# Short-lag products of the second image held back for the last attention chunks and the first ffn group (one Trainium2 core)

## The chip, the cores and the metric

The kernel runs on one core of one Trainium2 chip. The metric is the device time of one execution in microseconds, the median of several runs. The engines are named as in the profile: PE (matrix multiply), PEld (its weight loads), DVE (vector), ACT (scalar), POOL (gpsimd) and SP (the queue that issues most DMAs).

## The reference, cut to what matters

Two images of 128 channels and 64 x 64 positions pass a neighbourhood-attention block (layer 0), then a layer 1 on their 4096 tokens. The change lies in layer 1:

```python
t = t + _L1_attn_ref(_ln_t(t))     # softmax(q q^T / sqrt(128), diagonal masked) q
t = t + _L1_ffn_ref(_ln_t(t), ...) # four branches on 1, 1/2, 1/4, 1/8 of the sequence, mixed by weights
def _stu(u, sigma, phi, Mu, Mpp, Mpm):
    return _compute_spectral(u, sigma, phi, Mpp, Mpm) + _compute_ar_u(Mu, u)
def _compute_ar_u(Mu, u):          # the short lags: three shifted products
    out = jnp.zeros(u.shape[:2] + (Mu.shape[-1],), dtype=u.dtype)
    for i in range(Mu.shape[0]):
        ui = jnp.pad(u, ((0, 0), (i, 0), (0, 0)))[:, :sl]
        out = out + jnp.einsum('btd,de->bte', ui, Mu[i])
    return out
```

`_compute_spectral` is a causal convolution of the tokens with 16 filters, followed by a matrix for each filter.

## The kernel before

Layer 0 takes roughly the first 450 us. Then `attention(0)` and `attention(1)` work the two images. An image's 4096 tokens are eight chunks of 512. The pairs (a, c) with c >= a are taken row by row: `weights` makes the scores (line 899) and their exponentials on ACT (906), `turned` transposes them (913, with a DVE copy that also sums rows, 916), and the products go into `own` (927) and `other` (952). When row a is done, DVE adds `own` to `xa` (931) and `fill(chunk, part)` is told. Rows get shorter: the seventh chunk (CHUNKS[6] = 6) is finished inside the last pair (7, 7), the eighth right behind it.

After each of the four steps of a pair `fill()` issues one step of other work: from the queue `urgent` if it has any, else from `steps`. A step that yields True lets the next queue have its turn in the same call. For each finished chunk `urgent` gets `after(b, c, part)`:

1. transpose the chunk's sum (976), divide by the softmax denominator and add to the tokens `tt` (981);
2. layernorm on DVE (174, 175, 164, 182) with a power on POOL (165), giving z; then a bare True;
3. transpose z (193) and copy it to `zc` on ACT (993);
4. and 5. products with the transform `tr` (1012), copied to `ub` (1014, three buffers) and stored to `us` in DRAM (1001);
6. the rest of the transform (1022, 1028, 1030).

After every fourth chunk a half h of the image is complete and `short_lags(b, h)` is due. It has eight steps: for each parity two steps that transpose four token tiles into `xa` (193 on `tt`, ACT copy 1044), then two products of three lags each on `zc` (1053, six matmuls) that DVE adds to `xa` (1060). For the second image the generator of half 0 is kept back (`kept`) until attention has ended. Its steps then alternate with the steps left over, which are the end of the seventh chunk, the eighth chunk and half 1.

`bank()` gives a PSUM tile from a pool of six, used by all of this. Outside blocks of `manual_schedule` a scheduler orders the instructions of each engine by program order and by its own estimate of when they are ready. [...]

The ffn follows, with PE in program order. `inputs(q)` reads `ut` back from `us` (1301), `blocks(q)` reads filter blocks `ct` (1254). `group()` makes 16 products `pc` (1320) that DVE and ACT copy to `y` (1321), and `project` multiplies them with the filter matrices (1332) into `acc`, which ACT copies to `ob` (1339). Two groups are made before the first projection. The PSUM pools of attention are closed before and new ones opened (`ps_c` of six tiles). The filter matrices are made in `filter_matrices` by DVE additions of weights that DMAs bring (1114, 1117, 1119, 1130 to 1135), as steps of the second attention.

`zc` is one tile in the pools of attention and serves both images. `tt[0]`, the first image's tokens, lives in a pool of its own, closed with them.

Of the kernel before, what the change touches and what calls it, by code (L numbers as in the profile page):

```python
# [8 lines left out]
F32 = mybir.dt.float32  # L9
# [5 lines left out]
P = 128  # L15
NB = 2
T = 4096
TH = T // 2
NT = T // P
# [76 lines left out]
def kernel(  # L96
# [20 lines left out]
    dram = ctx.enter_context(tc.tile_pool(name="dram", bufs=1, space=bass.MemoryType.DRAM))  # L117
    first_ = ExitStack()
    fp = first_.enter_context(tc.tile_pool(name="first", bufs=1))
    ap_ = ExitStack()  # L120
    tp0 = ap_.enter_context(tc.tile_pool(name="l1_t0", bufs=1, side="right"))

# [5 lines left out]


    tt, tok, cm = [None, None], [None, None], [None, None]
    tt[0] = tp0.tile([P, NT, P], F32, name="tt0")
    tok[0] = fp.tile([P, NT, P], F32, name="tok0")
    cm[0] = fp.tile([P, T], F32, name="cm0")

# [721 lines left out]
    with ap_:  # L858
# [17 lines left out]

        zc = tp.tile([P, 2, TH + 1], F32, name="zc")
        nc.gpsimd.memset(zc[:, :, 0:1], 0.0)  # L880

        def attention(b, fill):

# [85 lines left out]
        def after(b, c, part):  # L969

            n0 = 4 * c
            ph, f0 = divmod(n0, FB)
            par, h = divmod(ph, 2)
            pt = bank()
            for j in range(4):
                nc.tensor.transpose(pt[:, j * P : (j + 1) * P], xa[b][:, (n0 + j) * P : (n0 + j + 1) * P], ident)
            rden = sp.tile([P, 4], F32, tag="rden", name="rden")
            nc.vector.tensor_reduce(rden, part[:, n0 : n0 + 4, :], AX.X, ALU.add)
            nc.vector.reciprocal(rden, rden)
            for j in range(4):  # L980
                nc.vector.scalar_tensor_tensor(
                    tt[b][:, n0 + j, :], pt[:, j * P : (j + 1) * P], rden[:, j : j + 1], tt[b][:, n0 + j, :],
                    ALU.mult, ALU.add,
                )
            yield
            z = sp.tile([P, 4, P], F32, tag="z4", name="z4")
            layernorm(z, tt[b][:, n0 : n0 + 4, :])
            yield
            yield True
            pt = bank()  # L990
            transposed(pt, z)
            s0 = 1 + h * (TH // 2)
            nc.scalar.copy(
                zc[:, par, s0 : s0 + TH // 2].rearrange("p (c f) -> p f c", f=FB)[:, f0 : f0 + 4, :],
                pt.rearrange("p (f c) -> p f c", f=4),
            )
            yield
            z2 = z.rearrange("p f d -> p (f d)")

            def store(m0, q, src):  # L1000
                nc.sync.dma_start(
                    out=us[m0 // 2 : (m0 + P) // 2, :, 2 * h + q, f0 : f0 + 4, b, par, :].rearrange(
                        "g r f d -> (g r) f d"
                    ),
                    in_=src.rearrange("p (f d) -> p f d", d=P),
                )

            for m0 in (0, P):
                for q in range(2):
                    rows_ = slice(q * SB, (q + 1) * SB)  # L1010
                    pu = bank()
                    nc.tensor.matmul(pu, lhsT=tr[rows_, h, m0 : m0 + P], rhs=z2[rows_], start=True, stop=True)  # L1012
                    ub = sp.tile([P, 512], F32, tag="ub", name="ub", bufs=3)
                    (nc.scalar.copy if q else nc.vector.tensor_copy)(ub, pu)
                    store(m0, q, ub)
                yield

            banks = [bank() for q in range(2)]
            for i in range(2):
                for q in range(2):  # L1020
                    rows_ = slice(q * SB, (q + 1) * SB)
                    nc.tensor.matmul(
                        banks[q][i * 64 : (i + 1) * 64, 0:256], lhsT=tr[rows_, h, 2 * P : NC],
                        rhs=z2[rows_, i * 256 : (i + 1) * 256], start=True, stop=True,
                    )
            ub = sp.tile([P, 512], F32, tag="ub", name="ub", bufs=3)
            for q in range(2):
                (nc.scalar.copy if q else nc.vector.tensor_copy)(ub[:, q * 256 : (q + 1) * 256], banks[q][:, 0:256])
                for i in range(2):
                    nc.sync.dma_start(  # L1030
                        out=us[P:, :, 2 * h + q, f0 + 2 * i : f0 + 2 * i + 2, b, par, :].rearrange("g r f d -> (g r) f d"),
                        in_=ub[i * 64 : (i + 1) * 64, q * 256 : (q + 1) * 256].rearrange("p (f d) -> p f d", d=P),
                    )
            yield

        def short_lags(b, h):


            for par in range(2):
                n0 = (par * 2 + h) * FB  # L1040
                for f0 in range(0, FB, 4):
                    pt = bank()
                    transposed(pt, tt[b][:, n0 + f0 : n0 + f0 + 4, :])
                    nc.scalar.copy(xa[b][:, (n0 + f0) * P : (n0 + f0 + 4) * P], pt)
                    yield
                xv = xa[b][:, n0 * P : (n0 + FB) * P].rearrange("p (f c) -> p f c", f=FB)
                for c0 in range(0, P, 64):
                    py = bank()
                    for lag in range(3):
                        from_par = (par - lag) % 2  # L1050
                        back = (lag - par + from_par) // 2
                        s0 = 1 + (h * P + c0) * FB - back
                        nc.tensor.matmul(  # L1053
                            py, lhsT=mu[:, lag, :], rhs=zc[:, from_par, s0 : s0 + 512], start=(lag == 0), stop=(lag == 2)
                        )
                    pv = py.rearrange("p (c f) -> p f c", f=FB)
                    first = h == 0 and c0 == 0
                    for lo, hi, s in ((0, 32, 0), (32, 64, 1)) if first else ((0, 64, 2 + h),):
                        xs = xv[:, :, c0 + lo : c0 + hi]
                        nc.vector.scalar_tensor_tensor(  # L1060
                            xs, pv[:, :, lo:hi], seg[:, s : s + 1], xs, ALU.mult, ALU.add
                        )
                    yield
# [74 lines left out]
        def filters():  # L1138
# [44 lines left out]
            for slot in range(begin[-1] + SG):  # L1183
# [4 lines left out]
                    keep(*mj)  # L1188
                yield

        def filler(b, steps, kept=None):

            urgent, done = [], []

            def fill(c=None, part=None):
                if c is not None:
                    done.append(c)
                    urgent.append(after(b, c, part))
                    if len(done) % 4 == 0:
                        held = kept if kept is not None and len(done) == 4 else urgent  # L1200
                        held.append(short_lags(b, len(done) // 4 - 1))
                    return

                for queue in (urgent, steps):
                    while queue:
                        got = next(queue[0], False)
                        if got is None:
                            return
                        if got:
                            break  # L1210
                        queue.pop(0)

            return fill, urgent

# [23 lines left out]
        l1 = ctx.enter_context(tc.tile_pool(name="l1", bufs=1))  # L1238
        mpl = l1.tile([P, KF, P], F32, name="mpl")
        mmi = l1.tile([P, KF, P], F32, name="mmi")  # L1240
        inv = l1.tile([P, 3, CB], F32, name="inv")
        ctp = ctx.enter_context(tc.tile_pool(name="blocks", bufs=5))

# [17 lines left out]
                first_blocks.append(blocks(q))  # L1261
                yield

        steps = [*left, filter_matrices(mpl, mmi), load_blocks()]

        kept = []
        fill, left = filler(1, steps, kept)
# [1 line left out]
        for gen in steps:  # L1269
            for _ in gen:  # L1270
                pass
        kept = kept.pop()
        for gen in left:
            for _ in gen:
                next(kept, None)
        for _ in kept:
            pass

# [7 lines left out]
    outf = out.rearrange("b c h w -> b c (h w)")  # L1288
    with ExitStack() as cv:
        cp = cv.enter_context(tc.tile_pool(name="conv", bufs=5))  # L1290
        obp = cv.enter_context(tc.tile_pool(name="ob", bufs=1))
        ps_c = cv.enter_context(tc.tile_pool(name="ps_c", bufs=6, space=PSUM))
        ps_p = cv.enter_context(tc.tile_pool(name="ps_p", bufs=2, space=PSUM))

        ob = obp.tile([P, 2, NB, FB, 2 * BC, 2], F32, name="ob")
        ob_last = obp.tile([P, 2, NB, FB, BINS - 2 * BC, 2], F32, name="ob_last")

        def inputs(q):

# [4 lines left out]
            )  # L1304
            return ut

        def group():


            y = cp.tile([P, 8, KF, 2, 32], F32, tag="y", name="y", bufs=2)  # L1310
            for q in range(GB // 2):
                ct, ut = ahead.pop(0)
                for par in range(2):

                    cv_ = ct[:, :, 0 : 288 + par * 32].rearrange("p o (l c) -> p o l c", l=2)[:, :, :, 0 : FB * KF]
                    for b in range(NB):
# [44 lines left out]
        ahead = [(ct, inputs(to_load.pop(0))) for ct in first_blocks]  # L1361
        rest = []
        with tc.manual_schedule(engines={mybir.EngineType.PE}):
            y = group()
            for g in range(BINS // GB):
                following = group() if g + 1 < BINS // GB else None
                acc = ps_p.tile([P, 64 * GB], F32, tag="acc", name="acc")
# [140 lines left out]
```

## Time and profile before

| | |
|---|---|
| median of 3 runs | 2209.53 us (2209.5 to 2211.03) |
| profiled execution: time, span | 2211.93 us, 2210.2 us |
| mean granted PE clock | 0.992 |
| PE busy | 2156.2 us, 98% of the span |
| DVE, ACT, POOL busy | 938.0, 780.6, 278.5 us |
| second attention begins, ffn begins | about 817 us, 1306.33 us |

The profile is of one execution; a view by stretches gives, for each stretch of time, each engine's busy time with its number of instructions, then the granted PE clock, the DMA engines' busy share and GB/s. The chain of waits goes back from the last instruction to what released it, and is shown here in order of time: start, length, engine, tile and line. "issue" there is time for which the profile shows no wait. A line number can be that of a helper: 193 is any group of transposes.

### The profile page before, as it was taken

The numbers are of one execution on the slowest core, as the hardware profiler recorded it, in microseconds if no ns is written. First come the engines' busy times: TensorE is split into PE (matmuls) and PEld (weight loads), VectorE is DVE, ScalarE is ACT, GpSimd is POOL, SyncE is SP. The second block draws the span as 40 slices with busy tenths as digits, with TensorE's granted clock in tenths as the row PEclk, the third lists the DMA queues.
The fourth block names the chain that finished last, engine by engine and source line by source line (L and its number), as shares of the span: only waits on it lengthen the run. The fifth ranks groups of instructions, "written<-read, shape, count | busy, mean of one in ns | idle before, by whom it ended". The sixth has DMA issues, their size and how long they took to land.

```text
span 2210.2 us, 31763 instructions
## 1 busy us (share of the span) xinstructions
PE 2156.2 (98%) x11920; PEld 1335.0 (60%) x11920; DVE 938.0 (42%) x3054; ACT 780.6 (35%) x1904; POOL 278.5 (13%) x355
## 2 busy tenths in 40 slices
PE   7899998999999998999999999999999999999998
PEld 4677765544554444544544447767767676777776
DVE  5899985434443346433333442232222323232232
ACT  3898883222333222222223232232222323232232
POOL 3477874200000000000000000000000000000000
PEclk8999999999999999999999999999999999999999
DMA  4222212021000025000000141221212121212101
GB/s 147 61 62 61 62 50 52 0 77 43 24 24 25 24 68 156 24 25 24 0 25 24 48 111 40 59 52 47 59 44 55 43 56 43 57 42 57 40 10 77
DMA packets 170345, 110.54 MB, mean 50 GB/s; under 512 B 21311, under 2 KB 155087, under 8 KB 169680
## 3 DMA queue, kind: packets, MB, share of 16 engines
q1 hardware_dynamic: 169266, 105.01, 17.8%
q8 instruction: 94, 1.54, 0.3%
q0 software_dynamic: 576, 2.10, 0.3%
q10 hardware_dynamic: 350, 1.41, 0.3%
q14 instruction: 59, 0.48, 0.1%
HBM read 73.86 MB, written 34.63 MB: 49 GB/s over the span
## 4 chain that ended last, share of the span: by engine, by line
PE 88%; DVE 5%; POOL 3%; DMA 2%; ACT 1%; issue 1%; SPq 1%; POOLq 0%; DVEq 0%; ACTq 0%
PE acc L1332 25%; PE pc L1320 13%; PE own L927 11%; PE bank L899 11%; PE other L952 8%; PE bank L913 4%; PE bank L333 2%; PE bank L1053 2%; PE bank L193 1%; PE bank L543 1%; PE bank L1012 1%; PE py L1354 1%; PE bank L507 1%; DMA st<-in_m_minus_dram 1%; PE po L565 1%; DVE ln_st L379 1%
## 5 line engine op out<-in xcount | busy, mean ns | idle before, releaser
L1321 DVE COPY y<-pc 128x512 f32<-128x512 f32 x320 | 221.6, 692 | 351.5 <-PE pc L1320 347.8
L906 ACT ACTIVATE e<-bank 128x512 f32<-128x512 f32 x288 | 171.8, 597 | 516.2 <-PE bank L899 387.8
L899 PE MATMUL bank<-cm 128*128 128x512 f32 x576 | 297.9, 601 | 1.4 <-DVE y L654 1.4
L1332 PE MATMUL acc<-y,mpl 128*128 128x256 f32 x1280 | 292.1, 382 | 0.0
L1332 PE MATMUL acc<-y,mmi 128*128 128x256 f32 x1280 | 288.0, 379 | 0.0
L1320 PE MATMUL pc<-ct,ut 64*128 64x512 f32 x1280 | 285.2, 595 | 0.9 <-issue 0.9
L1332 PEld LDWEIGHTS acc<-y,mpl 128*128 128x128 f32 x1280 | 238.1, 190 | 59.4 <-issue 29.6
L1332 PEld LDWEIGHTS acc<-y,mmi 128*128 128x128 f32 x1280 | 242.6, 190 | 32.6
L927 PE MATMUL own<-et,tok 128*128 128x512 f32 x448 | 228.5, 597 | 7.5 <-DVE part L916 7.4
L1321 ACT COPY y<-pc 128x512 f32<-128x512 f32 x320 | 205.1, 641 | 86.6 <-PE pc L1320 86.6
L952 PE MATMUL other<-e,tok 128*128 128x512 f32 x448 | 229.7, 594 | 0.0
L1320 PEld LDWEIGHTS pc<-ct,ut 64*128 64x128 f32 x1280 | 121.5, 187 | 145.8 <-issue 140.6
L916 DVE CUSTOM_DVE_ANT_0 et<-bank,one 128x512 f32<-128x512 f32 x224 | 145.5, 687 | 131.5 <-PE bank L913 131.4
L1339 ACT COPY ob<-acc 128x256 f32<-128x256 f32 x32 | 19.0, 595 | 387.0 <-PE acc L1332 387.0
L927 PEld LDWEIGHTS own<-et,tok 128*128 128x128 f32 x448 | 84.4, 191 | 117.5 <-issue 73.3
L952 PEld LDWEIGHTS other<-e,tok 128*128 128x128 f32 x448 | 85.2, 191 | 107.8 <-issue 106.0
L1356 DVE TENSOR_TENSOR xa<-py,xa 128x512 f32<-128x512 f32 x32 | 22.1, 692 | 281.4 <-PE py L1354 281.4
L913 PEld LDWEIGHTS bank<-ident,e 128*128 128x128 f32 x896 | 102.9, 141 | 55.4 <-issue 47.0
L899 PEld LDWEIGHTS bank<-cm 128*128 128x128 f32 x576 | 94.5, 191 | 67.9 <-issue 44.7
L165 POOL TENSOR_TENSOR ln_rs<-ln_rs,mhalf 128x4 f32<-128x4 f32 x24 | 24.5, 1020 | 837.1 <-DVE ln_rs L164 837.1
L530 ACT ACTIVATE p<-p,mn 128x196 f32<-128x196 f32 x256 | 114.4, 449 | 14.3 <-DVE mn L520 13.8
L913 PE MATMUL bank<-ident,e 128*128 128x128 f32 x896 | 117.2, 274 | 0.0
(210 smaller groups left out, 2289.3 us busy)
## 6 DMA issues: line engine op xcount, KB each, us to landing
ut<-us SPq DMA_DIRECT2D x80, 256.0 KB
us<-ub SPq DMA_DIRECT2D x64, 256.0 KB
vw<-vd SPq DMA_DIRECT2D x256, 49.0 KB
ct<-gs SPq DMA_DIRECT2D x160, 72.0 KB
ct<-gs SPq DMA_DIRECT2D x160, 64.0 KB
gs<-sum SPq DMA_DIRECT2D x20, 256.0 KB
vd<-v SPq DMA_DIRECT2D x128, 32.0 KB
st<-in_m_plus_dram SPq DMA_DIRECT2D x16, 256.0 KB
```

Of the source, the lines that this page charges most:

```text
L333: nc.tensor.matmul(pl, lhsT=wg[:, lo : lo + P], rhs=zT, start=True, stop=True)
L530: nc.scalar.activation(p, p, AF.Exp, bias=t[name + "mn"][:, h : h + 1], scale=-1.0, accum_out=t["den"][:, u, h : h + 1],)
L899: nc.tensor.matmul(ps, lhsT=cm[b][:, n * P : (n + 1) * P], rhs=cm[b][:, chunk(c)], start=True, stop=True)
L906: nc.scalar.activation(e, ps, AF.Exp, bias=0.0, scale=ASCALE, accum_out=part[:, n, c : c + 1])
L913: nc.tensor.transpose(pt[:, k * P : (k + 1) * P], es[k][:, m * P : (m + 1) * P], ident)
L916: nc.vector.tensor_tensor_reduce(et, pt, one, 1.0, 0.0, ALU.mult, ALU.add, part[:, n, a : a + 1])
L927: nc.tensor.matmul(own, lhsT=tok[b][:, n, :], rhs=e, start=first, stop=last)
L952: nc.tensor.matmul(other, lhsT=tok[b][:, 4 * CHUNKS[a] + j, :], rhs=es[j], start=(j == 0), stop=(j == 3))
L1053: nc.tensor.matmul(py, lhsT=mu[:, lag, :], rhs=zc[:, from_par, s0 : s0 + 512], start=(lag == 0), stop=(lag == 2))
L1320: nc.tensor.matmul(pc, lhsT=ut[fp, b, par, :], rhs=cv_[fp], start=True, stop=True)
L1321: (nc.scalar.copy if f else nc.vector.tensor_copy)(y[:, 4 * f : 4 * f + 4, :, par, b * 2 * FB + q : (b + 1) * 2 * FB : 2], pc.rearrange("p ...
L1332: nc.tensor.matmul(acc, lhsT=(mmi if l else mpl)[:, k, :], rhs=y[:, 1::2, k, ::-1, :] if l else y[:, 0::2, k, :, :], start=(l == 0 and k = ...
```

## The change

`short_lags` now does its four transposing steps first and its four products after them. For the second image the first four steps of each half are queued as urgent work (`residual_of`), and only the products are kept. Of half 0's four, one is issued by `fill` in the last pair, after seven finished chunks, where the queue yields True, and three stand behind steps 1, 2 and the bare True of the eighth chunk. Of half 1's four, two are issued before the attention pools close, and two inside the first `group`, one ahead of each parity of its first input, in a bank of `ps_c`.

To let products run after the attention pools are closed, the second image has its own `zc[1]`, laid over the first image's token tile `tt0`, whose pool now closes after the first group, and its own copy `mu1` of the lag matrices, made by POOL. `ob` and `ob_last` are allocated after that.

```diff
-        zc = tp.tile([P, 2, TH + 1], F32, name="zc")
-        nc.gpsimd.memset(zc[:, :, 0:1], 0.0)
+        zc = [tp.tile([P, 2, TH + 1], F32, name="zc"), tt0.rearrange("p (s t) -> p s t", s=2)]
+        nc.gpsimd.memset(zc[0][:, :, 0:1], 0.0)
...
                     yield
+            for par in range(2):
+                n0 = (par * 2 + h) * FB
                 xv = xa[b][:, n0 * P : (n0 + FB) * P].rearrange("p (f c) -> p f c", f=FB)
                 for c0 in range(0, P, 64):
-                    py = bank()
+                    py = lag_bank()
...
-                            py, lhsT=mu[:, lag, :], rhs=zc[:, from_par, s0 : s0 + 512], start=(lag == 0), stop=(lag == 2)
+                            py, lhsT=(mu1 if b else mu)[:, lag, :], rhs=zc[b][:, from_par, s0 : s0 + 512], start=(lag == 0), stop=(lag == 2)
...
+        def residual_of(lags):
+            for _ in range(4):
+                next(lags)
+                yield
...
-                        held = kept if kept is not None and len(done) == 4 else urgent
-                        held.append(short_lags(b, len(done) // 4 - 1))
+                        lags = short_lags(b, len(done) // 4 - 1)
+                        if kept is not None:
+                            kept.append(lags)
+                            lags = residual_of(lags)
+                        urgent.append(lags)
...
+                if kept and len(done) == 7:
+                    next(kept[0], None)
...
+        def for_lags():
+            nc.gpsimd.memset(zc[1][:, :, 0:1], 0.0)
+            nc.gpsimd.tensor_copy(mu1, mu)
+            yield True
+
+        steps = [*left, for_lags(), filter_matrices(mpl, mmi), load_blocks()]
...
-        kept = kept.pop()
         for gen in left:
-            for _ in gen:
-                next(kept, None)
-        for _ in kept:
+            for i, got in enumerate(gen):
+                if got or gen is left[-2] and i < 2:
+                    next(kept[0], None)
+        for _ in kept[0]:
             pass
+        lags = kept[1]
+        for _ in range(2):
+            next(lags)
...
-        def group():
+        def group(other=None):
...
                 for par in range(2):
+                    if other:
+                        next(other, None)
...
-            y = group()
+            y = group(lags)
+            lags_.close()
```

## The prediction

> **What bounds the kernel now.** I read the page first, then the stretches by time, then the chain of waits and the DMA queue between the last attention chunk and the first ffn group. The page's first part:
>
> ```profile
> PE 2156.2 (98%) x11920; PEld 1335.0 (60%) x11920; DVE 938.0 (42%) x3054; ACT 780.6 (35%) x1904; POOL 278.5 (13%) x355
> ```
>
> PE is busy 98% of the span, and the edit removes no matmul. It can only win where PE stands still or runs at a lower clock. From 885 us to the start of the ffn at 1306 us, PE's only gaps over 0.05 us lie behind 1260 us: 0.36 and 0.78 before line 927 inside the last attention pairs, then the three that the stretches below show (from, to; length, PE busy; the column before the DMA share is the granted clock):
>
> ```profile
> 1267.91:1269.51 1.60, 0.00 (x1) 0.04 (x1) 1.19 (x3) 0.00 (x0) 1.01 (x1) 1.00 0.00 0
> 1269.51:1271.13 1.62, 1.62 (x8) 0.82 (x8) 0.62 (x3) 0.58 (x1) 0.00 (x0) 1.00 0.00 0
> 1271.13:1274.54 3.41, 3.41 (x12) 1.22 (x8) 0.69 (x1) 1.67 (x3) 0.00 (x0) 0.50 0.28 82
> 1274.54:1282.65 8.11, 8.11 (x38) 4.15 (x36) 4.77 (x17) 1.75 (x4) 0.00 (x0) 1.00 0.45 127
> 1282.65:1284.51 1.86, 0.00 (x0) 0.00 (x0) 0.64 (x5) 0.67 (x2) 1.01 (x1) 1.00 0.00 0
> 1284.51:1305.44 20.93, 20.92 (x72) 9.38 (x72) 6.38 (x12) 4.78 (x8) 0.00 (x0) 1.00 0.40 119
> 1305.44:1306.33 0.89, 0.00 (x1) 0.03 (x1) 0.75 (x1) 0.00 (x0) 0.00 (x0) 1.00 0.46 175
> ```
>
> The reader sees three holes (1.60, 1.86, 0.89) and one stretch of 3.41 us at half clock. The chain names what fills each hole:
>
> ```profile
> 1267.97 1.02 POOL ln_rs L165
> ...
> 1269.01 0.36 DVE z L182
> 1269.37 0.14 issue
> 1269.51 1.01 PE bank L193 x4
> ...
> 1281.82 0.75 DVE xa L1060
> ...
> 1300.28 5.15 PE bank L1053 x12
> 1305.44 0.89 issue
> 1306.33 14.00 PE pc L1320 x64
> ```
>
> Hole one is the layernorm of the seventh finished chunk (DVE statistics, the power on POOL, DVE z). Hole two is the same chain of the eighth; there a product's DVE addition (line 1060) had been queued ahead of the last statistics. Hole three is "issue" by name, but the DVE addition of the last product ends at 1306.23, and the first matmul of line 1320 starts 0.10 later: PE waits for a PSUM bank, not for data. The DMA queue:
>
> ```profile
> 1289.56 4.74 SPq L1001 DMA_DIRECT2D us<-ub  x4
> 1294.39 3.59 SPq L1030 DMA_DIRECT2D us<-ub  x4
> 1300.36 2.42 SPq L1301 DMA_DIRECT2D ut<-us  x5
> ```
>
> The ffn's inputs are read back from what the last chunk stored. PE's queue waited for the first of them for 3.35 us from 1299.6 (line 1320's own entry), so it was there at 1302.95. From the end of the last chunk's line 1022 (1293.23) to that input are 9.7 us, covered today by 12.1 us of short-lag work.
>
> **The change part by part.** The eight short-lag steps of an image half become four steps of four transposes (0.44 each when packed) and four products (six matmuls, 2.58 each: 5.15 for twelve). No count changes; only places do.
>
> (1) Transposes of half 0 move into attention, behind the fourth finished chunk: 4 x 0.44 = 1.74 us leave the tail and are paid there. PE is 100% busy in 1100:1200 and ACT 29%, so the four ACT copies (0.59 each) and the extra bank find room. They cost nothing net if ACT keeps up; ACT would have to be 2 to 3 us late before the exponentials, eight buffers deep, held PE. Taken as 0.
>
> (2) One product goes between the last two own matmuls of the last pair. PE then ends at 1267.07 + 2.58 + 0.86 = 1270.50 instead of 1267.91, and z, ready from 1269.37, is waited for no more: hole one (1.60) goes, and the four z transposes take 0.44 instead of 1.01: 0.57 more. The product's addition on DVE (two of 0.44) is ready at 1269.7, behind z; if it came first, z would be 0.9 late and a 0.5 us hole would stay.
>
> (3) Three products stand behind line 976 of the last chunk: 7.7 us of PE for a chain that needs 1.1 (line 981), 1.2 (statistics), 0.2, 1.1 (power), 0.4 (first z), about 4.1 with the handovers, or 6.4 with two additions of 0.75 queued in front and 0.8 of waiting for a store buffer. Hole two (1.86) goes, with 0.22 of piecewise transposes (0.66 against 0.44).
>
> (4) The last chunk's lines 1012, 1012, 1022 are now back to back. Their copies use three ub buffers, and the fourth copy needs the first store landed (for the seventh chunk 2.63 us from the store's issue at 1272.63 to ACT's copy at 1275.26). So the fourth bank comes free some 4.6 us after the start of 1012, and the fourth residual transpose, due at 4.0, stalls by about 0.65. The trace does not show this order: bounds 0 and 1.5, I take 0.4. Behind this wait on ACT stand the four residual copies (0.59 each), which nobody on PE needs before 10 us.
>
> (5) Two products and four transposes, then a third product in the new PSUM pool, stand ahead of the first line 1320: PE gets there 12.9 us after the last chunk's 1012 starts (2.71 for lines 1012 and 1022, 2.4 for the transposes with their stall, 7.74 for three products). The stores' chain gives 5.0 for the copies, 4.0 for four stores on SP and their landing, 2.7 for the read: 11.7. If a store takes 1.6 instead of 0.6, as one did today, 12.7. No wait, with a margin of 0.2 to 1.2; with no cover the whole 3 to 4 us would show.
>
> (6) The PSUM handover: the first tile of the new pool is now a product instead of line 1320. It waits 0 to 0.89, by the bank that it gets; I take 0.45. The two products inside the first group cost what they cost outside, plus two switches of 0.19 (2.77 against 2.58). DVE has 0.17 us idle in each 0.86 us of the group, and the additions find the room while the product holds PE.
>
> (7) POOL gets a memset and one copy of 384 columns; after the power at 838.8 its next work is the power at 948.0. The second zc lies in the first image's token tile, whose last reads are the transposes of half 1 (862 to 885 today), and its first write but for the memset follows that power at 948. ob is allocated later; its first write is one group later. All 0.
>
> **The clock.** A hole of 1.60, with the z transposes arriving piecemeal, was followed by 3.41 us at clock 0.50, which cost 1.7 us; the hole of 1.86 was followed by none. The Trainium skill, "TensorE: Matmul & The Clock Gate", Part 1, says that PE drops to half rate after at least one idle window of about 3.4 us, free-running. By that rule no hole here is long enough and closing them saves nothing of the clock; by the row it saves 1.7. The row decides for the profiled execution. But the page's free-running window fits that 1.86 did nothing, so I do not count on the half-clock stretch in each run: of the three timed runs two are at 2209.5 and one at 2211.0, a step of about that size.
>
> **The sum.** Gone: 1.60 + 0.57 + 1.86 + 0.22 + 0.89 = 5.1. New: 0.4 + 0.45 + 0.2 = 1.0. Net 4.1 without the clock, 5.8 with it. The profiled execution (span 2210.2, 2211.93 with what lies around it, 2.4 above the median) should become about 2206.1. For the median of 2209.53 I count a third of the 1.7: 4.7 less, 2204.8.
>
> **The rivals.** *Half the holes come back* (0.17): bank or ub wait of 1.5, first input 1 us late, a late z. Against it: each margin above is positive; for it: three are under 1.3 us and the instruction order is a scheduler's. Gain 2 to 3, about 2207.
>
> *The second attention's start is reordered, for the worse* (0.10). The largest hole of the trace is there:
>
> ```profile
> PE own L927 <- DVE part L916: 4.4, 1, 4.4
> 842.00:848.00 6.00, 6.00 (x11) 2.88 (x12) 3.03 (x8) 1.79 (x3) 0.00 (x0) 0.51 0.66 184
> ```
>
> On DVE, filter-matrix additions wait for their weights' DMA (3.23 at 831.8), and the row-sum copy that PE needs is queued behind; 6.8 us at half clock follow. The edit regroups the first image's last short lags (862 to 900) and puts a POOL step before the filter matrices. If that brings one more such hole, it costs 4.4 + 3.4 = 7.8, and 7.8 - 4.7 = 3.1 slower: 2212.6. It decides from a DVE delay that costs PE more than 4.7. Against: the program up to 862 is the same.
>
> *The same place, for the better* (0.10): the hole shrinks, 3 to 8 more saved, about 2199.
>
> *It moves work and hides nothing* (0.05): the scheduler places products elsewhere and the chains stay bare: 2209.5.
>
> **How the numbers follow.** The case above has 0.58; about three quarters of it lie beyond 0.2% (4.4 us, about what a measurement of this kernel can tell from no change), since 4.1 to 5.8 straddles that bound. Faster: 0.44 + 0.10 = 0.54; within: 0.14 + 0.17 + 0.05 = 0.36; slower: 0.10. The range 2200.5 to 2209.5 takes in the likeliest case, the half-closed holes and no gain, and leaves out the slower case and half of the better one.
>
> **What would show it.** Right: line 193 on z right behind line 927 with no wait; six matmuls of line 1053's product between the last own matmuls; three products before the last z; clock 1.00 throughout the tail; from 1263.77 to the end of the first group's products 4 to 6 us less. Wrong: a wait for line 1301's reads at the first line 1320, a hole over 1 us at the residual transposes, or other holes than 4.42, 0.55 and 0.85 between 830 and 890.

## The result and the profile after

| | before | after |
|---|---|---|
| median (22 runs each, taken side by side) | 2210.38 us (2208.23 to 2215.73) | 2206.64 us (2203.91 to 2211.38) |
| ratio | | 0.998, 95% interval 0.9974 to 0.9987 |
| profiled execution: time, span | 2211.93, 2210.2 us | 2206.54, 2204.8 us |

The kernel is faster by 3.7 us of 2210: less than the 4.7 forecast, inside the range. The interval of the ratio is 2.9 to 5.7 us, so the median alone does not show a shortfall; the profile does. In the changed kernel's file the lines stand a little lower: 193 is now 195, 927 is 929, 1053 is 1059, 1320 is 1346; the second image's residual transposes are still in the helper's line. Its page, first part:

```profile
PE 2153.3 (98%) x11920; PEld 1333.3 (60%) x11920; DVE 937.4 (43%) x3054; ACT 780.1 (35%) x1904; POOL 279.4 (13%) x357
```

PE's instructions are as many as before. The chain of waits in the same place, in order of time (start, length, engine, tile, line):

```profile
1266.22 2.58 PE bank L1059 x6
1268.79 0.86 PE own L929 x2
1269.65 0.44 PE bank L195 x4
...
1273.18 7.73 PE bank L1059 x18
1280.91 0.44 PE bank L195 x4
1281.35 1.11 PE bank L1014 x4
...
1283.16 2.32 DMA us<-ub
...
1285.79 0.60 ACT ub L1016
...
1286.43 0.67 PE bank L195 x4
...
1287.13 0.44 DVE ub L1030
...
1287.61 7.13 PE bank L1059 x12
...
1294.77 0.76 DVE xa L1066
...
1295.66 2.81 PE py L1059 x6
1298.47 1.92 PE pc L1346 x8
```

Read it from the top. A product stands between the last own matmuls and three stand before the last z transposes; both times line 195 follows line 929 or the product at once and takes 0.44. Holes one and two are gone. Then PE hangs on a store: DVE's copy (line 1016), 2.32 us of DMA, ACT's copy, and only then the residual transposes. It hangs once more on DVE's copy in line 1030 (the fifth store copy), and a third time on the addition (line 1066) of the last product before the new PSUM pool. The view by stretches gives first the whole tail (from the start of the last eight own matmuls to the first projection), then its three holes and the stretch at half clock among them:

```profile
1262.94:1315.31 52.37, 49.79 (x184) 22.09 (x184) 27.48 (x66) 16.69 (x27) 2.02 (x2) 0.97 0.36 100
1285.32:1286.43 1.11, 0.00 (x0) 0.00 (x1) 0.00 (x0) 0.64 (x2) 0.00 (x0) 1.00 1.04 308
1287.09:1287.61 0.52, 0.00 (x0) 0.00 (x0) 0.42 (x1) 0.52 (x2) 0.00 (x0) 1.00 0.53 156
1288.35:1291.76 3.41, 3.41 (x5) 1.35 (x4) 0.00 (x0) 0.48 (x1) 0.00 (x0) 0.50 0.33 82
1294.73:1295.66 0.93, 0.00 (x0) 0.03 (x1) 0.75 (x1) 0.00 (x0) 0.00 (x0) 1.00 0.69 238
```

The waits from 1283 us on (who <- whom: total, times, longest) give them their names:

```profile
ACT ub L1016 <- DMA us<-ub: 2.7, 1, 2.7
PE bank L195 <- ACT ub L1016: 1.1, 1, 1.1
PE py L1059 <- DVE xa L1066: 0.9, 1, 0.9
PE bank L1059 <- DVE ub L1030: 0.5, 1, 0.5
```

The same stretches of before are the measure: second attention's first row, a stretch of attention that holds the fourth chunk's end, and the tail.

```profile
811.07:943.76 132.69, 125.13 (x404) 59.71 (x404) 73.08 (x195) 32.35 (x86) 2.31 (x2) 0.97 0.33 93
1158.12:1205.47 47.35, 47.35 (x162) 22.94 (x161) 17.32 (x54) 13.48 (x36) 1.01 (x1) 1.00 0.10 28
1263.77:1320.26 56.49, 52.14 (x200) 24.44 (x201) 27.86 (x66) 19.13 (x31) 2.02 (x2) 0.97 0.34 93
```

And the first two of after:

```profile
809.55:941.18 131.63, 123.34 (x404) 59.39 (x404) 73.23 (x195) 32.50 (x86) 2.77 (x3) 0.99 0.33 94
1155.54:1204.64 49.10, 49.10 (x178) 24.60 (x177) 17.30 (x54) 15.82 (x40) 1.01 (x1) 1.00 0.09 27
```

The tail is 56.49 - 52.37 = 4.1 shorter. The sixteen matmul records that left it are the four residual transposes, and the attention stretch has become 49.10 - 47.35 = 1.75 longer by sixteen. So the tail's net gain is 2.4: 1.8 of holes (1.60 + 1.86 + 0.89 = 4.35 became 1.11 + 0.53 + 0.94 = 2.58), and a rest of 0.6, which fits the z transposes that no longer arrive piecemeal. The other 3 us of this one execution's 5.4 are in places that the tail's edit does not reach: 1.5 before 810 us, 1.1 in the second attention's start, where half-clock time went from 6.83 to 3.41, and 0.4 behind the first projection.

The second attention's start also has a cost of the change. POOL's copy of the lag matrices stands just ahead of the first chunk's layernorm power, and PE waits for that chunk's z. The first three lines are of after, the last of before:

```profile
813.76 0.50 POOL L1283 COPY mu<-mu 128x384 f32<-128x384 f32 x1 [22.01 <-PE own L929]
814.23 1.01 POOL L167 TENSOR_TENSOR ln_rs<-ln_rs,mhalf 128x4 f32<-128x4 f32 x1
PE bank L195 <- DVE z L184: 2.1, 1, 2.1
PE bank L193 <- DVE z L182: 1.6, 1, 1.6
```

PE's hole there went from 1.59 to 2.07 us. With the kernels of the experiments below, it is 2.06 or more in all eight that have the copy, and 1.59 or 1.60 in the three that have not.

### The profile page after: what moved, and what is told of

Read it like the earlier page. It is cut to its first block, busy times and chain, and to the rows that moved or that the text cites. A ratio compares the mean times of both kernels' runs of the same rounds, so it can differ in the third digit from the quotient of the medians.

```text
span 2204.8 us, 31763 instructions
## 1 busy us (share of the span) xinstructions
PE 2153.3 (98%) x11920; PEld 1333.3 (60%) x11920; DVE 937.4 (43%) x3054; ACT 780.1 (35%) x1904; POOL 279.4 (13%) x357
## 4 chain that ended last, share of the span: by engine, by line
PE 89%; DVE 4%; POOL 3%; DMA 2%; issue 1%; ACT 1%; ACTq 0%; SPq 0%; POOLq 0%; DVEq 0%
PE acc L1358 25%; PE pc L1346 13%; PE own L929 11%; PE bank L901 10%; PE other L954 8%; PE bank L915 4%; PE bank L335 2%; PE bank L1059 2%; PE bank L545 2%; PE bank L195 1%; PE bank L1014 1%; PE py L1380 1%; PE bank L509 1%; PE po L567 1%; POOL tok L706 1%
```

## The experiments

Open after this: are the tail's three new holes the store ring and the PSUM handover, and do they explain the whole shortfall; does each part of the change do what the prediction said; does regrouping the first image's short lags cost or bring anything.

**The stores' buffers.** The last two chunks' store copies take tiles from the exponentials' eight instead of the ring of three (`ub`, which the stores use in turn):

```diff
+            def store_tile():
+                if b and c in CHUNKS[6:]:
+                    return ep.tile([P, 512], F32, tag="e", name="e")
+                return sp.tile([P, 512], F32, tag="ub", name="ub", bufs=3)
...
-                    ub = sp.tile([P, 512], F32, tag="ub", name="ub", bufs=3)
+                    ub = store_tile()
```

> The changed kernel, with the store buffers of the second image's last two chunks taken from the exponentials' eight tiles instead of the ring of three. Theory A (the gain is made between 1263 us and the end of the first group, and three new holes take part of it back; two of them come from the ring of three): the holes of 1.11 before the fourth residual transposes and of 0.53 before the next product go to under 0.2 together, ACT no longer waits for the us stores there, the clock has no half-rate stretch after them; 1.5 to 3.3 us under the changed kernel in its profile, 5 to 7 under the kernel before. Rival B (the gain is made at the second attention's start, where short lags of the first image were regrouped; the tail is only moved): the holes may go, and the time stays near 2206.6. Rival C (the fourth transposes wait for ACT's order, not for the ring): the hole of 1.1 stays.

Measured: 2203.88 us against 2209.95, ratio 0.9974 (0.9964 to 0.9984). Its chain from the last chunk's projections on (lines here are five higher: 1059 is 1064, 1014 is 1019):

```profile
1283.60 1.92 PE bank L1019 x8
1285.51 0.59 PE bank L1029 x8
1286.11 1.90 PE bank L195 x16
1288.00 5.17 PE bank L1064 x12
...
1294.09 2.81 PE py L1064 x6
```

The sixteen residual transposes now run in one piece, 1.90 for all, right behind line 1029, and two products right behind them; the holes of 1.11 and 0.53 are gone, and with them the half clock behind them. Only the addition before the new pool (0.94) is left. The median is 2.8 us under the changed kernel's, but the intervals overlap (0.9964 to 0.9984, and 0.9974 to 0.9987): that the holes go is shown by the trace, how much time that brings is less certain.

**The PSUM pool.** The bank pool of attention lives on and serves the ffn too, so that no pool is closed and opened between the products:

```diff
-        ps_m = ap_.enter_context(tc.tile_pool(name="l1_ps_m", bufs=6, space=PSUM))
+        ps_m = ctx.enter_context(tc.tile_pool(name="l1_ps_m", bufs=6, space=PSUM))
...
-        ps_c = cv.enter_context(tc.tile_pool(name="ps_c", bufs=6, space=PSUM))
...
-            return ps_c.tile([P, 512], F32, tag="pc", name="py")
+            return ps_m.tile([P, 512], F32, tag="bank", name="py")
```

> The changed kernel with the six PSUM tiles of attention kept open through the ffn, so that the products inside the first group take the next tile of the same ring instead of the first tile of a new pool. Theory A: the hole of 0.94 before the third product of half 1 goes, about 0.9 us less; the holes of 1.11 and 0.53 stay. If that hole is not the opening of a new pool but the wait for the bank of the product just before, it stays with a kept pool too, or moves by one product. Rival B: nothing visible in the time either way.

Measured: 2206.04 us against 2209.95, 0.9984 (0.9978 to 0.9991); no difference from the change itself can be told. The waits of its tail say why:

```profile
DVE ub L1030 <- DMA us<-ub: 4.5, 1, 4.5
PE bank L1059 <- DVE ub L1030: 1.9, 1, 1.9
```

The product's wait on the addition is gone: the handover was that. But the fifth store copy, DVE's in line 1030, came later, and so the product that takes its bank stood for 1.9 us instead of 0.5. One hole went, and another grew by more than that.

The growth need not be the pool's doing. The trace also records when each semaphore, the counter that a waiting engine watches, is counted up. By these records the fifth copy waits for the chunk's second store, here as in the changed kernel, and a store's landing has 16 steps. Here the second store was issued at 1284.90; 15 steps were done at 1287.66, and the last at 1289.57. In the changed kernel the last step came at 1286.91, 0.5 behind the others; without the product in the last pair (below) it came with them, at 1287.30, and there is no second hole. So the first hole, 1.10 or 1.11 in four traces with the ring of three, is the ring itself; the second is the ring and a late step, and its size differs from trace to trace. What makes the step late was not tested. In these traces a single packet of the queue that the profile calls q8 instruction is under way shortly before the late step or during it, here from 1287.58 to 1288.54.

**Both edits together.** 

> Both edits together on the changed kernel. Theory A: no hole over 0.2 us between the last own matmul and the first projection, no half-clock stretch there; 2.5 to 4.3 us under the changed kernel's profile, a ratio to the kernel before of about 0.997. Rival B: about 2206 as the changed kernel.

Measured: 2204.24 us, 0.9973 (0.9963 to 0.9983). Its tail, and that of the kernel with the wide buffers alone, one line from each kernel's view by stretches:

```profile
1265.84:1313.57 47.73, 47.46 (x185) 21.66 (x185) 27.75 (x66) 16.92 (x27) 2.02 (x2) 1.00 0.39 110
```

```profile
1265.18:1313.74 48.56, 47.62 (x184) 21.50 (x185) 27.73 (x66) 16.92 (x27) 2.01 (x2) 1.00 0.40 108
```

With both, PE stands 0.27 us in 47.73. That hole lies before the group's first matmul, and PE's queue (the third number is the longest wait, in ns) had stood there for the first input:

```profile
L1350 PEldq EVENT_SEMAPHORE  x5: 51/51/4464, 1291.8 to 1299.4; - x5
```

By the semaphore records that input landed at 1296.25; PE was done with the product ahead of it at 1296.40 and began the group at 1296.66. So once the other holes are gone, the chain of store and read is the next to hold PE, and the product inside the group covers most of it: without that product PE would have been there at 1293.81. The tail is 0.8 shorter than with wide buffers alone, but the medians do not show it; at 0.04% that is below what these runs can tell.

**The product in the last pair.** Left out; it then follows the three of the eighth chunk, still ahead of the second half's products and the ffn:

```diff
-                if kept and len(done) == 7:
-                    next(kept[0], None)
```

> The changed kernel without the one product inside the last attention pair (that product then follows at the end of half 0's). Theory A: the hole before the z transposes of the seventh chunk comes back, 1.6 us, with 0.5 us of piecewise transposes, 1.5 to 2.2 us more than the changed kernel; if clock follows holes, a half-rate stretch (1.7 us) may come behind it. Rival B: same time as the changed kernel.

Measured: 2207.80 us, 0.9995 (0.9987 to 1.0003). Hole one is back (first line), and the stall at the residual transposes stays (second):

```profile
1268.38:1269.98 1.60, 0.00 (x1) 0.03 (x1) 1.18 (x3) 0.00 (x0) 1.01 (x1) 1.00 0.00 0
1286.22:1287.32 1.10, 0.00 (x1) 0.00 (x0) 0.00 (x0) 0.64 (x2) 0.00 (x0) 1.00 0.93 293
```

At full clock its tail is 1.6 longer than the changed kernel's (52.3 against 50.7). This execution has no half clock in the tail, behind the same hole of 1.60 that was followed by 3.41 us of it in the kernel before.

**No product beside the eighth chunk's norm.** The three products are issued only after that chunk:

```diff
-            for i, got in enumerate(gen):
-                if got or gen is left[-2] and i < 2:
-                    next(kept[0], None)
+            for _ in gen:
+                pass
```

> The changed kernel with the three products taken out of the last chunk's norm; they follow behind its stores, ahead of half 1's products. Theory A: from line 978 to the z transposes PE stands still for 6 to 7 us (7.7 of cover less what the chain leaves over), so 6 to 7 us more than the changed kernel, and with a hole that long a half-clock stretch of 3.4 (1.7 us) behind it: 2212 to 2215, slower than the kernel before. Rival B: under 1 us more.

Measured: 2212.99 us against 2210.34, 1.0013 (1.0006 to 1.0019): slower than the kernel before. Its largest wait of PE, DVE's line 1030 in its timeline (start, length; in brackets the idle time before it and its releaser), and the stretch at half clock:

```profile
PE bank L195 <- DVE z L184: 6.3, 1, 6.3
```

```profile
1275.82 0.42 DVE L1030 COPY ub<-bank 128x256 f32<-128x256 f32 x1 [1.75 <-DMA us<-ub]
```

```profile
1275.57:1285.81 10.24, 5.78 (x20) 2.22 (x20) 4.99 (x19) 2.07 (x4) 1.01 (x1) 0.50 0.32 92
```

The bare chain leaves PE idle for 6.35 us, and 5.78 us of work at half rate go with it, which cost 2.9. About 4.1 of the 6.35 is the chain as the prediction counted it; the rest is DVE, which stood at line 1030 for a store buffer, with the chunk's attention output (line 983) queued behind. The changed kernel has that wait of 1.75 too, under its three products. This is the part that carries the change: it hides a chain that costs more than the whole gain.

**No product inside the first group.** The two are done before it, so that the group is as before:

```diff
-        for _ in range(2):
-            next(lags)
+        for _ in lags:
+            pass
```

> The changed kernel with all four products of half 1 issued before the attention pools close, none inside the first ffn group. Theory A: the group's share hides nothing (the first input is there some 4 us before PE asks for it in the changed kernel), so the time is the changed kernel's within 1 us; the wait for the new pool's first tile moves to the first line 1320 and stays near 0.9. If the two products inside the group do cover the input's load, a wait for it of 1 to 3 us appears there.

Measured: 2208.10 us against 2210.34, 0.9994 (0.9985 to 1.0002). PE's waits, and its tail:

```profile
PE bank L1059 <- DVE ub L1030: 1.9, 1, 1.9
...
PE pc L1346 <- issue: 0.9, 1, 0.9
```

```profile
1268.89:1323.28 54.39, 50.50 (x185) 23.75 (x185) 27.50 (x66) 16.86 (x27) 2.01 (x2) 0.94 0.35 97
```

The handover's wait has only moved to line 1346, 0.89 as before the change; again the fifth store copy came 1.4 later. It is the second store's last step again (1294.23, the other 15 at 1292.34). That the two products stand inside the group and not ahead of it hides little that can be seen: 6.83 us of this tail ran at half clock, 0.86 of them a hole, so at full clock (work at half rate counted half) it is 54.39 - 2.98 = 51.4, the changed kernel's 52.37 - 1.70 = 50.7; the late step alone is 1.4. Its median is 1.5 us above the changed kernel's, in the traces by the clock more than by the work; the intervals just meet, so that stays open. Whether the products cover the input's load this run can't tell, since here too they all stand ahead of it.

**The first image alone.** The kernel before, with four transposing steps and then four products for the first image only:

```diff
-            for par in range(2):
...
+            if b:
+                return
+            for par in range(2):
+                n0 = (par * 2 + h) * FB
```

> The kernel before with one part of the change alone: the first image's short lags do four transposes and then four products; nothing else. Theory A: no change, within 0.5 us in the stretch 811 to 944 us and in the whole. Rival B (the gain is made at the second attention's start): 2 to 4 us less than before, with other holes between 830 and 890.

Measured: 2210.61 us against 2210.34, 1.0004 (0.9996 to 1.0012): nothing. Its second attention's start:

```profile
810.43:945.39 134.96, 126.24 (x405) 60.42 (x405) 73.27 (x195) 32.24 (x86) 2.31 (x2) 0.96 0.33 92
```

At full clock this is 130.5, before 129.7; the 0.8 fits its last hole there, 1.95 instead of 0.85, which is 1.26 in a kernel whose code is the same at that place (the next run), so it may be chance. Its tail has the three old holes (54.90 us) and, in this execution, no half clock behind them.

**Wide store buffers in the kernel before.** The first edit, made there.

> The kernel before with the wide store buffers for the second image's last two chunks. Theory A: ACT's wait of 1.7 for the us stores at 1273.6 goes, but PE was waiting for nothing behind it, so the tail's holes of 1.60, 1.86 and 0.89 stay and the time is that of before within 0.5 us: the ring became a limit only by the change. If the wide ring helps by itself, 1 to 2 us less.

Measured: 2210.35 us, 1.0003 (0.9996 to 1.0011). The old order had nothing to gain from buffers: its holes are

```profile
PE bank L193 <- DVE z L182: 3.5, 2, 1.9
PE pc L1325 <- issue: 0.9, 1, 0.9
```

as ever. The store stall belongs to the change, and the 6 us of the changed kernel with wide buffers come from the two together.

**An attempt at a better version.** Both edits, and the arithmetic of the filter matrices in the second attention's start moved from DVE to POOL, to shorten the 4.4 us hole there (`mixed` takes an engine; on POOL the fused multiply and add becomes two instructions):

```diff
-        def mixed(dst, src):
+        def mixed(dst, src, eng=nc.vector):
...
+                        eng.tensor_scalar(st2, st2, wt[:, i : i + 1], None, ALU.mult)
+                        eng.tensor_tensor(dst2, st2, dst2, ALU.add)
...
-                    mixed(dst[:, k0 : k0 + 4, :], src[:, k0 : k0 + 4])
+                    mixed(dst[:, k0 : k0 + 4, :], src[:, k0 : k0 + 4], nc.gpsimd)
```

> The changed kernel with wide store buffers and kept PSUM tiles, and with the filter matrices mixed on POOL instead of DVE (the fused multiply-add becomes a multiply and an add). It tests the price that the slower rival put on a hole at the second attention's start. If DVE's wait for the weights' DMA is what holds PE at 837 us, the hole of 4 us and the half-clock stretch behind it (6.8 us) go: up to 4 + 3.4 + 1.7 for the smaller holes at 860 to 876, so 5 to 9 us under the version with both edits, about 2196 to 2199. Against: POOL also makes the powers of the layernorms in order, and behind a mix that waits for its DMA the power at 838 comes later; then a z is late instead and the gain is 0 to 3.

Measured: 2209.94 us against 2209.46, 1.0005 (0.9996 to 1.0013). The same kernel without the move had 0.9973 against the kernel before; its median, of other runs on another chip, is 5.7 us lower. The waits at that place and POOL's timeline (start, length, line, operation):

```profile
DVE z L184 <- POOL ln_rs L167: 11.4, 1, 11.4
PE own L929 <- DVE part L918: 10.2, 1, 10.2
```

```profile
845.63 1.56 POOL L1128 TENSOR_SCALAR mpl<-st,wt 128x512 f32<-128x512 f32 x1
847.16 1.04 POOL L167 TENSOR_TENSOR ln_rs<-ln_rs,mhalf 128x4 f32<-128x4 f32 x1
```

The layernorm's power stood in POOL's queue behind the mixes; without the move it ran at 838.7. DVE's z waited for the power, the row sum behind z on DVE, and PE for the row sum: the hole grew from 4 us to 10.2. So the version to keep, by the traces, is the change with wide store buffers, with or without the kept pool (0.9974 and 0.9973).

The tails side by side, in us; the third column counts work at half rate half:

| | tail | at full clock | holes |
|---|---|---|---|
| before | 56.49 | 54.8 | 1.60, 1.86, 0.89 |
| after | 52.37 | 50.7 | 1.11, 0.53, 0.94 |
| wide buffers | 48.56 | 48.6 | 0.94 |
| kept pool | 52.59 | 50.9 | 1.10, 1.92 |
| both | 47.73 | 47.7 | 0.27 |
| no product in the pair | 52.34 | 52.3 | 1.60, 1.10, 0.94 |
| none in the group | 54.39 | 51.4 | 1.10, 1.90, 0.89 |

## Why the prediction was right, and where its sum was not

**Steps 2 and 3, holes one and two: right.** In the changed kernel both are gone, with the piecewise transposes. Take out step 2 and hole one returns at 1.60; take out step 3 and a hole of 6.35 appears: the chain of 4.1, and some 2 of waiting for a store buffer, where step 3 had 0.8 for that.

**Step 1: right, exactly.** 1.75 us were paid in attention for the 1.74 named, and PE had no wait there (49.10 busy of 49.10).

**Step 4, the stores' ring: the mechanism right, the size wrong.** Taken as 0.4, within 0 to 1.5; it measured 1.11 + 0.53 = 1.64, and wide buffers remove all of it. The working itself had 0.65 for the fourth residual transpose (its bank free after 4.6, due after 4.0) and took less. The bank came free 5.08 after the start of line 1014 (1281.35 to 1286.43), and the transpose was due after 3.97: a stall of 1.11. And the working stopped at the fourth copy. The fifth, line 1030, is in the same ring, and the next product takes the bank that DVE empties there: 0.53 more in this execution, where the store's last step came 0.5 late.

**Step 6, the handover: at its upper end.** Taken as 0.45, within 0 to 0.89; it measured 0.94. The first tile of the new pool waits for the last user of the old one, here the addition of the product just before: with the pool kept it goes, with no product in the group it falls on line 1346. It is 0.89 or 0.94 in all eight profiled kernels that open a new pool there; the smaller waits that step 6 allowed for did not occur.

With these two terms put right, 4.1 - 1.24 - 0.49 = 2.4, which is the tail's net gain by the stretches.

**Step 7, POOL's copy: wrong.** It was taken as 0, since POOL's next work after the power at 838.8 is at 948.0. But the copy ran before that, at 813.76, just ahead of an earlier power, and PE's hole behind it grew by 0.48. No run leaves the copy out, but the holes with and without it agree to 0.01 in ten of the eleven traces.

**Step 5: right, for another reason.** Line 1346 waits for no input. SP's queue shows the read of the first input issued when PE still stood in the products:

```profile
1291.72 2.23 SPq L1325 DMA_DIRECT2D ut<-us  x5
```

By the semaphore records it landed at 1294.36, and PE asks at 1298.5. The margin is 4 us, not 0.2 to 1.2: the input came 13.0 after the start of line 1014, where the step had 11.7, but the stalls, the handover and the half clock made PE later still, 17.1 instead of 12.9. The input was there before the first product inside the group began (1295.66), so in this kernel the group's share covers nothing. With both later edits it does, and there the step's sum is nearly met: the input 12.0 after the start of the projections, PE 12.2.

**The clock: half right.** The stretch at half clock was expected to go and did not: PE ran 3.41 us at 0.50 behind 1.11 + 0.53, as it had behind 1.60. In the tails, holes of 1.1 to 2 us did it in some executions (1.60: in the kernel before with either kind of store buffers, not in the two other kernels with the same hole), holes of under 1 us in none, and the stretches are 3.41, 6.83 or 10.24 long. The Trainium skill, "TensorE: Matmul & The Clock Gate", Part 1, asks for an idle window of 3.4 us first, which none of these holes fills. So the row was right that short holes cost clock; and the page's free-running window fits that the moment matters. In each trace the stretches begin a whole number of steps of 3.413 us apart, in the changed kernel 841.20 and 1288.35, 131 steps. But what decides stays open: in the kernel before, the 1.86 lay whole within one step and had no half clock behind it.

Each run also lists its mean granted clock, from which the time lost to half rate is span x (1 - clock). It is coarse for a single run (0.001 is 2.2 us), less so for means: before 16.6 +/- 0.3 us lost and 2193.6 +/- 0.2 left, after 14.8 +/- 0.4 and 2192.3 +/- 0.3, with wide buffers 14.3 +/- 0.6 and 2189.8 +/- 0.6. Of the change's gain about 1.3 would be work and holes, and 1.8 clock. These runs of before are not the ones taken beside the changed kernel, whose clocks are not on record, and another 17 runs of before, on another chip, lost 15.1 +/- 0.7 with 2194.3 +/- 0.6 left. So the split is a rough one. That the 1.3 is less than the tail's 2.4 has one cause in sight, POOL's copy with 0.48; at full clock the second attention's start took 129.7 before and 129.9 after.

**The profiled execution** came out near the 2206.1 forecast at 2206.54, but not by the forecast's terms: the tail gave 2.4 net and no clock, and the rest came from before 810 us and from the second attention's start. That the totals agree is luck, and no proof of the sum.

**The rivals.** Half the holes coming back is what happened in the tail (2.58 of 4.35), at nearly its price: 2207 forecast for it, 2206.64 measured. Of the signs named for the wrong case two came: a hole over 1 us at the residual transposes (1.11), and other holes between 830 and 890 (4.30, 0.25 and 1.52 for 4.42, 0.55 and 0.85). The second attention's start was neither better nor worse by a whole hole, and the first image regrouped alone changes nothing in the median. How dear a longer hole is, the attempt with POOL showed: longer by 6 us, for about as much in the median. That the moved work hides nothing falls with steps 2 and 3.

## What to carry to other kernels

When filler work closes a hole, list what the instructions that now stand close together share, a ring of store buffers above all: a copy that waits for a store holds a PSUM bank, and the matmul that waits for the bank is where it shows. Count the evacuation after the store's landing, and every copy in the ring, not just the first. Where a pool is closed and another opened, put no evacuation directly ahead of the handover, or keep one pool. And place even a half-microsecond instruction on an idle engine with care: POOL was idle for 22 us before the copy, and the next thing it had to do was on PE's path.

## What the runs showed of the hardware that was not expected

- Half clock came in steps of 3.413 us on a fixed grid within each trace (in the kernel before, the stretches at 335.88, 841.05 and 1271.13 are 148 and 126 steps apart). Holes between 1.1 and 2.1 us were followed by it in some executions and not in others, while no tail with holes of only 0.94 or 0.27 (at most 0.8 before them) had any. One step costs 1.7 us of work, here behind holes of 1.6 to 2.1 in sum.
- A store of 128x512 float32 can have 15 of its 16 landing steps done and the last 1.9 us later (1287.66 and 1289.57 with the pool kept). Whoever waits for the buffer waits for the last.
- POOL took 1.56 us for a multiply by a column and 1.26 to 1.29 for an addition of 128x512 float32, so a mix of two instructions takes nearly 3 us there, and a power of 1 us queued behind such mixes ran at 847.2 where it had run at 838.7.
